# Involution weights made in the partition of their input column and copied from SBUF to SBUF, in a quantized-convolution and involution kernel

## The chip, the cores and the metric

The kernel runs on one core of a Trainium2 chip. The metric is the device time of one execution in microseconds; of three timed runs the median was 1388.15 us (1385.45 to 1391.19). The profile that this document quotes is one more execution, of 1388.26 us.

A core has a matrix engine (TensorE; the profile calls its matmuls PE and its loads of the stationary operand PEld), a vector engine (DVE), a scalar engine (ACT), GpSimd (POOL) and a queue engine (SP), each with its own instruction stream, and 16 DMA engines that all queues share. SBUF has 128 partitions; a matmul reads both operands from SBUF and writes PSUM. [...]

## The reference

The input is 32 images of 256 channels by 32 x 32 pixels, fp32. Two residual layers follow one another.

```python
# layer 0: group norm, 3x3 convolution with fp16-like quantization, bias, residual
x = x + _L0_conv_ref(_gn(x), weight, bias)
# layer 1: group norm, then an involution (7x7, 16 groups of 16 channels), residual
xn = _gn(x)
y = relu(bn(einsum('oc,bchw->bohw', w1, xn)))       # 64 features at each pixel
w = einsum('oc,bchw->bohw', w2, y) + b2             # 784 = 16 groups * 49 taps, at each pixel
patches = 7x7 neighbourhood of xn, zero padded
out = einsum('bgkhw,bgckhw->bgchw', w.reshape(b, 16, 49, 32, 32), patches)
x = x + out
```

The involution is a 7 x 7 convolution whose weights differ from pixel to pixel: each pixel has 49 weights for each of 16 groups, computed from its own 64 features `y`, and every channel of a group uses the same 49.

## The kernel before, in words

**The involution as a matmul.** The kernel turns the sum around: 128 *input* pixels (8 rows by 16 columns, one "side" of a block of 8 rows) stand on the partitions. The stationary operand is the input pixels' channels (`pixels`, a 64 x 32 corner of the array for each of two row halves and four groups), the moving operand is a "band": for each input pixel the weights with which it enters the output pixels around it. The matmuls of `sums` (line 517) add into PSUM tiles `acc`, and `add_windows` (line 533, DVE) adds these into the image in SBUF. An image has K = 4 blocks of 8 rows, each with SIDES = 2 sides of 16 columns, so 8 calls of `sums` of 32 matmuls each. Every fp32 matmul appears in the trace as two records, each with its own load.

**How a band comes about.** A weight is made where its *output* pixel is, and the band needs it where its *input* pixel is. `weights(b, r0)` (line 414) takes four rows of the image at a time: for each of them the 32 pixels' features are the stationary operand (64 features x 32 pixels), and two of the seven horizontal taps (224 columns of `w2_sb`; 112 for the last, single tap) are the moving operand. Four horizontal tap pairs fill the four 32-column strips of the array, and two rows its two 64-row halves, so eight such matmuls run side by side; a call has 16 matmuls (32 records) and an image eight calls. The result stands in PSUM with partition = strip of taps x column of the output pixel. `evict` (line 438, DVE, with the bias added) writes it into `w_sb`, a ring of 24 rows, 1920 instructions in all.

`scatter` (line 479) then sends each block of eight rows to DRAM: seven DMAs per block on SP's queue, each from 32 partitions, in pieces of 640 bytes, into the tensor `wd`, which is laid out by the column of the input pixel. `load_bands` (line 492) fetches the band of a block from there: 16 DMAs per block, each of 16 runs of 4512 bytes (70.5 KB), 14 of them issued by POOL and 2 by SP. The diagonal of the convolution (row r of the block shifts its weights by r) lies in the source's row step.

**The order of the work.** The whole order is written out by hand, in steps; an image has 16 of them. In step n, `front` of up to four later images advances by a stage (group norms on ACT and DVE, the 3x3 convolution on PE at line 336, nine matmuls a stage, then the features `y` through lines 384 and 391, and transposes into `pixels` at 399 and 403); on even steps follows `sums` of the current image and `weights` of a later one; on odd steps `add_windows`. Relative to the first `sums` of image b (step 0), `weights(b)` runs on the even steps -18 to -4 (`LEAD = 18`), the scatter of a block a step or two after its last rows, and `load_bands(b, k)` at step 4k - 9: the lag is 3 - 4 * NBAND with three band buffers. `sums` of the first side of a block waits for all DMAs of its band, so nothing on PE passes it.

**Queues.** POOL issues nothing but its share of the band loads. SP issues, in program order, image loads (line 108), scatters, its share of the band loads and stores (line 538). On each of the two queues a DMA waits for the eighth before it to land.

Of the kernel before, what the change touches and what calls it, by code (L numbers as in the profile page):

```python
# [9 lines left out]
F32 = mybir.dt.float32  # L10
AF = mybir.ActivationFunctionType
ALU = mybir.AluOpType

P = 128
B, C, H, W = 32, 256, 32, 32
N = H * W
# [41 lines left out]
S = H + 2 * PAD1  # L58
# [4 lines left out]
ROW = S * WPIX  # L63
WR = 4
NBAND = 3
SHARE = 8
NPIX = 6
RING = 24
FRONT = -56
LOAD = -63  # L70
LEAD = 18


@with_exitstack
def tile_quant_conv_then_involution(
# [23 lines left out]
    dram = ctx.enter_context(tc.tile_pool(name="dram", bufs=1, space=bass.MemoryType.DRAM))  # L99
# [43 lines left out]
    y_sb = [const.tile([P, N // 2], F32, name=f"y_{i}") for i in range(2)]  # L143
    bands = [const.tile([P, SIDES, WINC * WB + PAD], F32, name=f"band_{i}") for i in range(NBAND)]
    for t in bands[CH:]:
        nc.gpsimd.memset(t, 0.0)
    pixels = [const.tile([P, 2, PAIRS, PAIR], F32, name=f"pixels_{i}") for i in range(NPIX)]
# [4 lines left out]
    w_sb = const.tile([P, 2, RING, A, WIN, V], F32, name="w_sb")  # L152
    wd = dram.tile([H, S, WPIX], F32, name="wd")
# [4 lines left out]
    for kh in range(CH):  # L158
        wf = bands[kh].rearrange("p d n -> p (d n)")[:, : K0 * K0 * C].rearrange("p (k c) -> p k c", c=C)
        nc.sync.dma_start(wf, w0[kh * P : (kh + 1) * P])  # L160
        staged.append(wf)
# [3 lines left out]
    b2_sb = const.tile([P, 2, 2, SW], F32, name="b2_sb")  # L165
    for dj in range(K1):
        t, e = divmod(dj, 2)
        for r in range(2):
            nc.sync.dma_start(b2_sb[t * TW : (t + 1) * TW, e, r], b2[dj].partition_broadcast(TW))
# [19 lines left out]

    for col, cols, at, n in (  # L190
        (0, S, K1 * WB, PAD),
        (PAD1, PAD1, 0, PAD1 * WB),
        (W, PAD1, (K1 - PAD1) * WB, PAD1 * WB),
    ):
        to = bass.AP(
            tensor=wd.tensor,
            offset=wd.offset + col * WPIX + at,
            ap=[[ROW, H], [WPIX, cols], [1, n]],
        )
        nc.sync.dma_start(to, bands[NBAND - 1][:H, 0, :n].unsqueeze(1).to_broadcast([H, cols, n]))  # L200
# [87 lines left out]
    def front(b):  # L288
# [102 lines left out]
        nc.scalar.activation(y_sb[b % 2], py, AF.Relu, bias=bn_shift, scale=bn_scale)  # L391
# [14 lines left out]
    def weights(b, r0):  # L406

        pws = [ps_w.tile([P, 2, 2, SW], F32, tag=f"pw{i}", name=f"pw{i}") for i in range(2)]
        for r in range(2):
            for t in range(T):  # L410
                for i in range(2):
                    half = slice(i * CR, (i + 1) * CR)
                    dj = slice(2 * t, min(2 * t + 2, K1))
                    nc.tensor.matmul(  # L414
                        pws[i][t * TW : (t + 1) * TW, : dj.stop - dj.start, r],
                        y_sb[b % 2][half, (r0 // 2 + r) * W : (r0 // 2 + r + 1) * W],
                        w2_sb[half, dj],
                        start=True,
                        stop=True,
                    )  # L420
        for i in range(2):
            for e in range(2):
                p = P if e == 0 else (K1 // 2) * TW
                for r, rows, d0, d1, at in ring_pieces(b, r0 + 2 * i):
                    evict(pws[i][:p, e, r : r + rows], e, r, rows, d0, d1, at)

    def evict(of, e, r, rows, d0, d1, at):

        p = of.shape[0]
        to = w_sb[:p, e]  # L430
        to = bass.AP(
            tensor=to.tensor,
            offset=to.offset + at * WB + V * (K1 - 1 - d0),
            ap=[to.ap[0], [V * WIN, rows * A], [WB - V, d1 - d0], [1, V]],
        )
        of = of.rearrange("p r (a d v) -> p (r a) d v", a=A, v=V)
        bias = b2_sb[:p, e, r : r + rows].rearrange("p r (a d v) -> p (r a) d v", a=A, v=V)
        nc.vector.tensor_tensor(to, of[:, :, d0:d1], bias[:, :, d0:d1], ALU.add)  # L438

    def ring_pieces(b, r0):  # L440

        def place(r, d):
            s = r0 + r + d - PAD1
            return (b * H + s) % RING if 0 <= s < H else None

        def together(d):
            return place(0, d) is not None and place(1, d) == place(0, d) + 1

        pieces = []
        for rows, ok in (
            ((0, 2), together),
            ((0, 1), lambda d: place(0, d) is not None and not together(d)),
            ((1, 1), lambda d: place(1, d) is not None and not together(d)),
        ):
            d = 0
            while d < K1:
                d0 = d
                while d < K1 and ok(d) and place(rows[0], d) == place(rows[0], d0) + d - d0:  # L460
                    d += 1
                if d > d0:
                    pieces.append((*rows, d0, d, place(rows[0], d0)))
                else:
                    d += 1
        return pieces

    def scatter(b, k, part):

        at = (b * H + k * TR) % RING  # L470
# [161 lines left out]
```

## Time and profile before

| | before |
|---|---|
| timed runs, median (range) | 1388.15 us (1385.45 to 1391.19) |
| profiled execution: its own time, and the span of its instructions | 1388.26 us, 1386.5 us |
| PE / PEld busy | 1265.7 us (91%) / 809.6 us (58%) |
| DVE / ACT / POOL busy | 861.2 us (62%) / 727.1 us (52%) / 1010.0 us (73%) |
| DMA moved | 369.97 MB, 267 GB/s; queue shares 57.6% (SP) and 33.8% (POOL) of 16 engines |
| first and last start of `sums` (line 517) | 93.9 us and 1380.8 us |
| mean granted PE clock | 0.98 |

The page shows one execution on the chip. "Busy" of an engine counts its instructions' time; a group's line gives the source line, the engine, the shapes (output partitions x elements <- input), how often, its busy time and the mean of one in ns, and after the bar the idle time ahead of it and what ended that. Records of matmuls overlap, since each includes its way through the array, so the mean of one is longer than the pace at which they follow one another; the pace is read from the chain of the work that ended last, in order of time, which counts each stretch of time once. The share of a DMA queue is the time of its packets over the span of 16 engines.

### The profile page before, as it was taken

Reading aid. Unit: us, or ns where it says so; the run is one execution under the profiler, and the core shown is the slowest. Engines: PE = TensorE matmul, PEld = TensorE weight load, DVE = VectorE, ACT = ScalarE, POOL = GpSimd, SP = SyncE. Lnnn points to the kernel's source line nnn. Section 1 sums busy time; section 2 is a strip of 40 time slices with the busy share of each in tenths; the row PEclk is TensorE's granted clock in tenths of the full one; section 3 lists DMA queues with packets and bytes.
Section 4 is the critical chain, followed back from the end, with each engine's and each line's share of the span. In section 5 each row is a group of like instructions: output and inputs, shape, how many; then the busy total and the mean of one; then the engine's idle time right before and its main releaser. Section 6 shows DMA issues by size and latency. Waiting matters only on the chain.

```text
span 1386.5 us, 70020 instructions
## 1 busy us (share of the span) xinstructions
PE 1265.7 (91%) x29440; PEld 809.6 (58%) x29440; DVE 861.2 (62%) x3179; ACT 727.1 (52%) x1699; POOL 1010.0 (73%) x1818
## 2 busy tenths in 40 slices
PE   4799999999999999999999999999999998999763
PEld 2356666666665655566566666656666665656542
DVE  3366666666666666676676666657666675766542
ACT  4765555465646545665455565645556564553300
POOL 9067677687777777777768687777787767778785
PEclk9999999999999999999999999999999999999987
DMA  6089999999999999999999999999999999999995
GB/s 220 2 223 283 282 272 289 281 267 297 277 268 282 285 281 274 278 282 272 289 280 282 284 276 276 286 287 268 280 303 272 283 286 276 276 275 271 269 268 170
DMA packets 366568, 369.97 MB, mean 267 GB/s; under 512 B 78960, under 2 KB 308528, under 8 KB 366000
## 3 DMA queue, kind: packets, MB, share of 16 engines
q1 hardware_dynamic: 280240, 235.90, 57.6%
q0 software_dynamic: 86016, 129.60, 33.8%
q8 instruction: 234, 3.83, 1.2%
q14 instruction: 78, 0.64, 0.2%
HBM read 184.43 MB, written 180.76 MB: 263 GB/s over the span
## 4 chain that ended last, share of the span: by engine, by line
PE 58%; DMA 24%; POOL 5%; issue 4%; DVE 3%; ACT 3%; SPq 2%; POOLq 0%; DVEq 0%; ACTq 0%
PE pc L336 22%; PE acc L517 19%; DMA band<-wd 13%; PE pw L414 11%; DMA wd<-w_sb 9%; POOL band L492 5%; PE py L384 3%; PE pt L399 3%; DVE w_sb L438 2%; ACT junk L223 1%; SPq L479 1%; DMA w_sb<-in_w 1%; DVE x L533 0%; ACT xn L282 0%; DMA x<-in_x 0%
## 5 line engine op out<-in xcount | busy, mean ns | idle before, releaser
L492 POOL DMA_DIRECT2D band<-wd x1792 | 978.0, 548 | 363.0 <-DMA band<-wd 218.5
L438 DVE TENSOR_TENSOR w_sb<-pw,b_sb 128x16 f32<-128x16 f32 (+9 forms) x1920 | 373.7, 265 | 423.9 <-PE pw L414 403.5
L336 PE MATMUL pc<-xq,wq 128*128 128x496 f16 (+3 forms) x2304 | 535.8, 379 | 27.4 <-ACT xq L282 23.8
L517 PE MATMUL acc<-band,pixels 64*32 64x190 f32 (+1 forms) x16384 | 427.1, 330 | 68.5 <-DMA band<-wd 45.8
L336 PEld LDWEIGHTS <-wq 128*128 128x128 f16 x2304 | 206.8, 98 | 322.6 <-issue 110.1
L517 PEld LDWEIGHTS acc<-band,pixels 64*32 64x32 f32 x16384 | 301.7, 106 | 157.9 <-issue 86.1
L414 PE MATMUL pw<-w_sb,y 64*32 64x224 f32 (+1 forms) x8192 | 292.9, 332 | 17.0 <-issue 15.2
L533 DVE TENSOR_TENSOR x<-acc,x 128x380 f32<-128x380 f32 (+1 forms) x512 | 262.7, 513 | 32.8 <-PE acc L517 23.9
L414 PEld LDWEIGHTS pw<-w_sb,y 64*32 64x32 f32 x8192 | 187.7, 106 | 48.3 <-issue 31.1
L403 ACT COPY pixels<-pt 128x512 f32<-128x512 f32 x128 | 73.7, 576 | 237.5 <-PE pt L399 237.5
L223 ACT ACTIVATE junk<-x 128x512 f16<-128x512 f32 (+1 forms) x192 | 146.4, 763 | 20.1 <-DVE x L352 8.4
L223 ACT ACTIVATE junk<-x,mean 128x1024 f16<-128x1024 f32 x128 | 147.1, 1149 | 4.3
L254 ACT ACTIVATE s<-back,eps 128x2 f32<-128x2 f32 x64 | 18.9, 296 | 204.8 <-DVE back L239 204.7
L350 DVE TENSOR_SCALAR q<-pc 128x512 f16<-128x512 f32 x128 | 87.2, 682 | 19.3 <-PE pc L336 19.2
L282 ACT ACTIVATE xn<-x,off,rstd 128x512 f32<-128x512 f32 x128 | 96.2, 800 | 0.0
L352 DVE SCALAR_TENSOR_TENSOR x<-q,bias_sb,x 128x512 f32<-128x512 f16 x128 | 94.7, 740 | 0.3
L399 PEld LDWEIGHTS pt<-ident,xn 128*128 128x128 f32 x512 | 63.7, 142 | 25.9 <-issue 3.2
L399 PE MATMUL pt<-ident,xn 128*128 128x128 f32 x512 | 77.8, 275 | 0.1
L282 ACT ACTIVATE xq<-x,off,rstd 128x1024 f16<-128x1024 f32 x64 | 75.7, 1227 | 0.5 <-PE pc L336 0.5
L384 PEld LDWEIGHTS py<-xn,w_sb 128*64 128x64 f32 x2048 | 62.7, 138 | 16.6 <-issue 7.5
L244 ACT ACTIVATE mean<-back 128x2 f32<-128x2 f32 x64 | 12.7, 198 | 111.5 <-DVE back L239 111.4
L384 PE MATMUL py<-xn,w_sb 128*64 128x64 f32 x2048 | 67.6, 224 | 2.6 <-ACT xn L282 1.9
(40 smaller groups left out, 370.8 us busy)
## 6 DMA issues: line engine op xcount, KB each, us to landing
wd<-w_sb SPq DMA_DIRECT2D x896, 160.0 KB
band<-wd POOLq DMA_DIRECT2D x1792, 70.5 KB, 4.9
x<-in_x SPq DMA_DIRECT2D x64, 512.0 KB
out<-x SPq DMA_DIRECT2D x64, 512.0 KB
band<-wd SPq DMA_DIRECT2D x256, 70.5 KB
band<-in_w SPq DMA_DIRECT2D x2, 1152.0 KB
w_sb<-in_w SPq DMA_DIRECT2D x2, 196.0 KB
wd<-band SPq DMA_DIRECT2D x2, 180.0 KB
```

Source lines behind the costliest of these rows:

```text
L223: nc.scalar.activation(junk[:, n0:n1], src[:, h, n0:n1], func, bias=bias, accum_out=self.sums[:, i : i + 1])
L282: nc.scalar.activation(dst, src, AF.Identity, bias=self.off[:, one], scale=self.rstd[:, one])
L336: nc.tensor.matmul(pc.rearrange("p (r c) -> p r c", c=W)[:, r0 - nt * RT : r1 - nt * RT, c0:c1], wq[:, kh, k, mh * P : (mh + 1) * P], xq[: ...
L350: nc.vector.tensor_scalar(q, pc, F16_MAX, -F16_MAX, ALU.min, ALU.max)
L352: nc.vector.scalar_tensor_tensor(xt[:, mh, cols], q, bias_sb[:, mh : mh + 1], xt[:, mh, cols], ALU.add, ALU.add)
L384: nc.tensor.matmul(py[i * CR : (i + 1) * CR, cols], w1_sb[:, kh, :], px[:, r : r + 2], start=kh == 0, stop=kh == CH - 1,)
L399: nc.tensor.transpose(pt[:, i, h * P : (h + 1) * P], xn[:, h, (m + i) * P : (m + i + 1) * P], ident)
L414: nc.tensor.matmul(pws[i][t * TW : (t + 1) * TW, : dj.stop - dj.start, r], y_sb[b % 2][half, (r0 // 2 + r) * W : (r0 // 2 + r + 1) * W], w ...
L438: nc.vector.tensor_tensor(to, of[:, :, d0:d1], bias[:, :, d0:d1], ALU.add)
L492: queue.dma_start(band[j::JC, :, j * WB : j * WB + WPIX], src)
L517: nc.tensor.matmul(at[t * TW : (t + 1) * TW, h, :, f - top : l - top], px[p, a, v * GC : v * GC + TW], of[:, :, a, f - top : l - top, v], ...
L533: nc.vector.tensor_tensor(x_at, of, x_at, ALU.add)
```

## The change

**Features shifted instead of weights.** The partition of a weight is now that of its *input* pixel from the start. For input pixel column j, the weight of horizontal tap dj is that of the output pixel at column j - dj + 3; so the features `y` are stored with three zero columns on either side, and the stationary operand of a matmul is a window of them that is shifted by dj. The taps of `w2` and `b2` are reversed to suit. The layout of `y` puts the image's four blocks of eight rows next to each other, so that one stationary operand holds 128 pixels: one row of each of the four blocks, all 32 columns (64 features x 128 pixels).

**An image at a time.** For each row position rho around a block (-3 to 10), and each of the seven dj, one matmul makes the weights of those vertical taps, d0 to d1, that fall into the block: the moving operand has (d1 - d0) * 16 columns, 16 to 112. That is 98 matmuls an image, 49 in each 64-row half of the array, in pairs that run in both halves. They are dealt out to eight units of 14, 7, 4, 10, 4, 3, 4 and 3 pairs (`UNITS`), at the steps 0, 2, 4, 6, 8, 10, 12 and 13 after -18 (`STEPS`): the last unit stands at step -5, one step earlier than the last call did. All four bands of an image need all eight units. The eviction writes 128 partitions, in 20 instructions an image, into `w_sb`, which now holds two images and no ring.

**No DRAM.** The scatter and `wd` are gone. `load_bands` copies from SBUF to SBUF: 32 DMAs per block, each from *one* partition (8 rows of 4512 bytes, 36 KB) to eight partitions, half of them issued by SP and half by POOL.

**What pays for the room.** Two bands instead of three (so `load_bands(b, k)` is issued at step 4k - 5), bands that share their columns between the two sides, and a smaller scratch area for the descriptors that POOL writes.

```diff
-S = H + 2 * PAD1
+BLK = 8
+QB = H // BLK
+YW = (W + 2 * PAD1) * QB
+YR = BLK // 2
-NBAND = 3
-SHARE = 8
+SCRATCH = 4096
+NBAND = 2
+SHARE = 2
-RING = 24
+UNITS = (
+    ((-3, 0, 7), (8, 0, 7)),
+    ((0, 0, 7),),
+    ((1, 0, 4),),
+    ((1, 4, 7), (9, 0, 7)),
+    ((5, 0, 4),),
+    ((5, 4, 7),),
+    ((4, 0, 4),),
+    ((4, 4, 7),),
+)
+STEPS = (0, 2, 4, 6, 8, 10, 12, 13)
...
-    y_sb = [const.tile([P, N // 2], F32, name=f"y_{i}") for i in range(2)]
-    bands = [const.tile([P, SIDES, WINC * WB + PAD], F32, name=f"band_{i}") for i in range(NBAND)]
+    y_sb = [const.tile([P, YR * YW + 2 * QB], F32, name=f"y_{i}") for i in range(2)]
+    bands = [const.tile([P, (WINC + WINI) * WB + PAD], F32, name=f"band_{i}") for i in range(NBAND)]
...
-    w_sb = const.tile([P, 2, RING, A, WIN, V], F32, name="w_sb")
-    wd = dram.tile([H, S, WPIX], F32, name="wd")
+    w_sb = const.tile([P, 2, BLK, WPIX], F32, name="w_sb")
...
-        nc.scalar.activation(y_sb[b % 2], py, AF.Relu, bias=bn_shift, scale=bn_scale)
+        to = y_sb[b % 2][:, QB : QB + YR * YW].rearrange("p (r c k) -> p r c k", r=YR, k=QB)[:, :, PAD1 : PAD1 + W]
+        of = py.rearrange("p (k r c) -> p r c k", r=YR, c=W)
+        nc.scalar.activation(to, of, AF.Relu, bias=bn_shift, scale=bn_scale)
...
+    def weights(b, n):
+        pws = [ps_w.tile([P, NT], F32, tag=f"pw{i}", name=f"pw{i}") for i in range(2)]
+        parts = [[], []]
+        muls = [[], []]
         for i in range(2):
+            at = 0
+            for rho, j0, j1 in UNITS[n]:
+                rho = BLK - 1 - rho if i else rho
+                d0, d1 = max(0, PAD1 - rho), min(K1, BLK + PAD1 - rho)
+                cols = (d1 - d0) * G
+                parts[i].append((at, rho, j0, j1, d0, d1))
+                for dj in range(j0, j1):
+                    muls[i].append((at, rho, dj, d0, d1))
+                    at += cols
+        for both in zip(*muls):
+            for i, (at, rho, dj, d0, d1) in enumerate(both):
+                half = slice(i * CR, (i + 1) * CR)
+                k, r = divmod(rho, BLK)
+                y0 = QB + (r // 4 * 2 + r % 2) * YW + dj * QB + k
+                nc.tensor.matmul(
+                    pws[i][:, at : at + (d1 - d0) * G].rearrange("p (a n) -> p a n", a=A),
+                    y_sb[b % 2][half, y0 : y0 + P],
+                    w2_sb[half, dj].rearrange("p (a n) -> p a n", a=A)[:, :, V * d0 : V * d1],
+                    start=True,
+                    stop=True,
+                )
+        for i in range(2):
+            for part in parts[i]:
+                evict(b, pws[i], *part)
...
+    def load_bands(b, k):
+        band = bands[(b * K + k) % NBAND]
+        for i in range(W):
+            d, j = i // JC, i % JC // 2 + i % 2 * JC // 2
+            w = w_sb[(d * JC + j) * QB + k : (d * JC + j) * QB + k + 1, b % 2]
+            src = bass.AP(
+                tensor=w.tensor,
+                offset=w.offset,
+                ap=[w.ap[0], [WPIX - V, TR], [1, WPIX]],
+            )
+            at = (j if d else WINI + j) * WB
+            to = band[j::JC, at : at + WPIX]
+            if i % SHARE == SHARE - 1:
+                nc.sync.dma_start(to, src)
+            else:
+                nc.gpsimd.dma_start(to, src)
...
-            if b is not None and i % 2 == 0:
-                weights(b, i // 2 * WR)
-
-            for part in range(2):
-                b, i = due(n, -LEAD + 1 + part)
-                if b is not None and i % 2 == 0:
-                    for k in range(K):
-                        if i // 2 == min((k + 1) * TR // WR, H // WR - 1):
-                            scatter(b, k, part)
+            if b is not None and i in STEPS:
+                weights(b, STEPS.index(i))
...
-    nc = bacc.Bacc("TRN2", target_bir_lowering=False, num_devices=1)
+    nc = bacc.Bacc("TRN2", target_bir_lowering=False, num_devices=1, dynamic_dma_scratch_size=SCRATCH)
```

The new `evict` differs from the old one in its strides alone: with d = d1 - d0 and q = 8 (j1 - j0), it adds `b2_sb` to 128 partitions of q * d pairs and writes these into the image's half of `w_sb`.

## The prediction, made before the changed kernel was run

> **What bounds the kernel now.** I read the page's busy shares first, then its chain, then the chain in order of time, then PE's waits.
>
> ```profile
> PE 1265.7 (91%) x29440; PEld 809.6 (58%) x29440; DVE 861.2 (62%) x3179; ACT 727.1 (52%) x1699; POOL 1010.0 (73%) x1818
> ...
> q1 hardware_dynamic: 280240, 235.90, 57.6%
> q0 software_dynamic: 86016, 129.60, 33.8%
> ```
>
> PE and the DMA engines (57.6% + 33.8%) are both near full, so the shares don't say which sets the time. The chain in order of time does:
>
> ```profile
> 980.13 2.01 PE pc L336 x9
> 982.14 2.02 PE py L384 x64
> 984.16 1.51 PE acc L517 x44
> 985.67 0.76 PE pw L414 x15
> 986.43 2.01 PE pc L336 x9
> 988.44 1.50 PE acc L517 x39
> ```
>
> It runs on PE, each piece starting where the last one ended; columns are start, length, work. An image is eight times (acc 1.50 + pw 0.75 + pc 2.01) = 34.1 us, plus py 2.02 and four stretches of pt. From the first `sums` (93.9) to the last (1380.8) an image takes 1286.9 / 32 = 40.2 us. So a microsecond of PE work per image costs 32 us, unless it falls into a wait. The waits on transfers are few:
>
> ```profile
> PE acc L517 <- DMA band<-wd: 45.8, 21, 7.5
> PE acc L517 <- DMA wd<-w_sb: 5.5, 1, 5.5
> ```
>
> That is 51 us in total (total, times, longest), all that lighter DMA can give back to PE directly, though the chain puts 24% of the span down to DMA: most of that lies beside a busy PE.
>
> **Weights on PE.** `weights` costs 0.75 us a call in the chain, 8 x 0.75 = 6.0 us an image. The streams explain it: two rounds, two records each, of 224 columns are 896 columns in 0.75 us, 0.84 ns a column; eight tiles run side by side, and a load of only 32 columns hides under 188 ns of streaming. After, 49 pairs of matmuls stand in two tiles of 64 x 128. Streaming shrinks a little: 3136 columns x 2 records x 0.84 = 5.3 us. But each record now needs its own load of 128 fp32 columns, and streams only 16 to 112. What does such a load take?
>
> ```profile
> L384 PE MATMUL py<-xn,w_sb x2048: 216/222/271, 56.3 to 1302.8; 128*64 128x64 f32 x187
> L414 PE MATMUL pw<-w_sb,y x32: 256/349/373, 61.1 to 61.7; 64*32 64x224 f32 x24, 64*32 64x112 f32 x8
> 631.56 0.60 PE L399 MATMUL pt<-ident,xn 128*128 128x128 f32 x4
> 632.09 1.41 PE L517 MATMUL acc<-band,pixels 64*32 64x133 f32 x60
> 60.77 0.38 PE L336 MATMUL pc<-xq,wq 128*128 128x496 f16 x1
> 61.09 0.98 PE L414 MATMUL pw<-w_sb,y 64*32 64x224 f32 x32
> ```
>
> The first two (by line: minimum/median/maximum) give the load where it lies bare, in the first record after a change of shape: 271 - 222 = 49 ns for 64 columns, 373 - 349 = 24 ns for 32 (the window of one call, the first). It grows by 25 ns per 32 columns, so 98 ns for 128. The next two (timeline) give the nearest shape: four records of pt, each a 128-column fp32 load and 128 columns of stream, in 632.09 - 631.56 = 0.53 us, of which 0.1 is the change of shape: 107 ns each. The change itself is in the last two: pc's last record starts at 60.77 and streams 2.01 / 9 = 0.22, pw starts at 61.09, 0.10 later. I take 107 ns a record, as nearest in shape; longest stream 112 x 0.84 = 94, so the load is always the longer. Both tiles load side by side: in that first call the eight tiles, two to each strip, show the same 373. An image: 98 x 0.107 = 10.5, and per unit 0.10 to enter the shape, which `weights` shared with `sums` before, and 0.07 for the last stream: 8 x 0.17 = 1.4. Together 11.9 us in place of 6.0: **+5.9 us, x 32 = +187 us**. Bounds: with loads hidden entirely 5.3 + 1.4 = 6.7, +22 us; with the tiles loading in turn (196 x 0.107 + 1.4 = 22.4), +525 us.
>
> [...]
>
> **Waits on transfers that go.** wd is written and read no more: 143 MB out and 147 in become 148 MB inside SBUF. The 51 us go: **-51 us**. Bounds 0 (another stall takes their place) and -51.
>
> **The last unit and the first band.** The wait that comes is this one. Until now block 0's band was fetched as soon as its rows were scattered. After, all 32 DMAs of (b, 0) wait for DVE's eviction of unit 7, at step -5, and the first `sums` of the image for all 32. On PE there stand between: py 2.02, sums 1.50, pc 2.01, sums 1.50, unit 0 of the next image (14 pairs, 28 x 0.107 + 0.17 = 3.2), pc 2.01: 12.2 us. On the other side:
>
> ```profile
> L438 DVE TENSOR_TENSOR w_sb<-pw,b_sb 128x224 f32<-128x224 f32 x256 | 98.1, 383 | 187.8 <-PE pw L414 184.7 <-DMA wd<-w_sb 3.0
> L438 DVE TENSOR_TENSOR w_sb<-pw,b_sb 128x64 f32<-128x64 f32 x64 | 13.7, 215 | 19.1 <-PE pw L414 18.7
> L492 POOL DMA_DIRECT2D band<-wd x1792: 547/547/683, 77.8 to 1372.9; - x200
> L492 SPq DMA_DIRECT2D band<-wd x256: 570/592/2219, 79.3 to 1361.6; - x128
> DMA to landing us min/median/max: 2.4/4.9/8.8
> ```
>
> Eviction: (383 - 215) / 160 = 1.05 ns an element, 148 fixed; unit 7 has two of 336 elements, 1.0 us, and 0.2 to wake. Then fifteen issues ahead of the last: 8.2 us on POOL at 547, 8.9 on SP at 592; the number of runs per DMA halves, so these are upper bounds (SP's scatters went at 302). Then landing, 2.4 to 4.9 us. Sum 11.8 to 15.0 against 12.2: PE waits 0 to 2.8 us an image, 0 to 87 us. With half the data per DMA and half the load I stand near the lower end: 0.8 us, **+25 us**. The bands k = 1 to 3 wait for `sums` of band k - 2 instead; from the end of `sums` 1 to the start of `sums` 4 lie three rounds of acc, pw, pc with pt, over 14 us even before units grew: nothing.
>
> **Queues.** POOL: 2048 DMAs at most 547 are 1120 us, 8.75 us a band against 45.9 / 4 = 11.5. SP loses 896 scatters and has 2048 band DMAs, 9.5 us a band at 592; loads of x, 63 steps ahead, queue behind them; the store ahead of band k = 1 makes SP wait for one `add_windows` (two of 513 ns), within that band's slack. Eight in flight a queue at 0.55 allow 4.4 us to land. Nothing, as long as DMAs land so; cover gone, see the third rival.
>
> **DVE, ACT, start.** 1920 evictions (374 us) become 640: 640 x 0.148 + 200,704 elements x 1.05 ns = 305 us. DVE is at 62%, and a unit has two steps of some 2.5 us to be emptied (unit 7 one, with pc and py between): nothing. y's 32 strided writes (769 ns each) lie stages ahead of use: nothing. w_sb's clearing grows with its columns from 6.5 to 15.3 us on POOL, long before the first weights at 61 us: nothing.
>
> **Sum.** Against the profiled execution's own 1388.3 us (0.1 above the median): 1388.3 + 187 - 51 + 25 = **1549, say 1550 us**, 12% slower. With loads at 98 ns it would be 1521; with the late band at 0 or 87 us, 1524 to 1611.
>
> **Rivals.**
> *Loads hide, nothing is late.* 1388 + 22 - 51 = 1359 us, 2% faster. For it: before, every load hid, and the waits on bands are real. Against it: 49 and 24 ns bare, and pt's 107. It decides where a record costs under 65 ns: 98 x 0.065 + 1.4 = 7.7, +54 us against the -51. 0.09.
> *Loads hide, the first band is late.* Unit 0 shrinks by 1.3 us, and PE's way to step 0 with it, to 10.9: the wait is 0.9 to 4.1 us, 28 to 127 us, so 1387 to 1486, middle 1435. 0.13.
> *One partition is too slow a source.* Every band DMA reads 36 KB from one partition; before, it read DRAM, and a scatter read 32 partitions. No row has one. The windows at the first scatters, with no band load yet, show what few partitions yield (DMA share and GB/s last):
>
> ```profile
> 71.00:72.50 1.50, 1.50 (x38) 0.82 (x37) 0.78 (x3) 1.37 (x3) 0.00 (x0) 1.00 0.89 186
> 72.70:73.70 1.00, 1.00 (x7) 0.44 (x6) 1.00 (x5) 1.00 (x2) 0.00 (x0) 1.00 1.01 270
> ```
>
> The first DMAs, from partitions 0 to 63, keep the engines 89% busy at 186 GB/s; when 64 to 127 join it is 270. So where the bytes stand limits. At worst a partition gives its share of 32, 186 / 32 = 5.8 GB/s: with sixteen in flight 93 GB/s, 12.4 us for the 1155 KB of a band, 128 x 12.4 + 95 = 1.68 ms. If a queue's DMAs went one at a time it would be worse, above 3 ms. Against it: neighbours in a queue read different partitions, and 102 GB/s would do. 0.18, half of it under 1.72 ms.
>
> [...]
>
> **How the numbers follow.** Forecast 0.60 (1500 to 1640), and 0.09, 0.13 and 0.18 as above. Low 1420 leaves out the first rival and a third of the second (0.04); high 1720 leaves out half of the third, 0.09. A change of under 0.5% (1381 to 1395) can't be told from none: same 0.03, from the second rival's edge; faster 0.09; slower 0.88.
>
> **What will show it.** `weights` on the chain at 0.21 us a pair, some 10 to 12 us an image, PEld busy through it; no DMA ahead of `sums` but at each image's first, under 2 us; DMA share near half; DVE near 790 us. I am wrong if a pair takes under 0.13 us (loads hide), if the waits ahead of all four bands grow (one partition too slow: landing above 5 us, queues waiting for their own DMAs), or if the granted clock falls below 0.96 during the sparse units.

## The result and the profile after

The changed kernel takes **1859.05 us** (median of 4 runs, 1852.52 to 1872.09) against 1387.31 us before: 1.341 times as long, with a 95% interval of 1.333 to 1.349. Forecast were 1550 us and a range of 1420 to 1720. The direction was right, the size was not: 472 us more, where 162 were forecast. Three executions of the experiments below, one of lead20's and two of both20's, took over 1.5% longer than the fastest of the same kernel and are left out of the medians.

The page of the changed kernel: busy time, granted clock (tenths, 40 slices), busy share of the DMA engines, and the two DMA queues (packets, MB, share of 16 engines).

```profile
PE 1612.6 (87%) x27520; PEld 1109.0 (60%) x27520; DVE 777.4 (42%) x1899; ACT 734.6 (40%) x1699; POOL 1121.6 (60%) x2075
...
PEclk9988899988889988889988889988889888888776
DMA  4077666676766667666677766667667667666665
...
q1 hardware_dynamic: 61168, 144.34, 34.8%
q0 software_dynamic: 65536, 74.12, 30.4%
```

The queues move 222.6 MB in place of 370 and yet hold the DMA engines for 65% of a longer span. The granted clock of TensorE, 0.98 on average before, is 0.875. DVE is at 777 us, as forecast (790).

The chain in order of time, around the first sums of an image (start, length, work):

```profile
924.94 3.26 PE pw L424 x56
928.20 2.02 PE pc L332 x9
930.22 0.23 issue
930.45 2.12 POOL band L465 x4
932.57 3.30 DMA band<-w_sb
935.88 2.79 PE acc L490 x49
938.66 3.18 PE pw L424 x28
941.84 3.88 PE pc L332 x9
...
946.56 1.52 PE acc L490 x44
948.09 1.05 PE pw L424 x16
949.14 2.01 PE pc L332 x9
```

Three things can be read here. A unit of weights with 14 pairs (L424 x56) costs 3.26 us for 28 records a tile, as the prediction had it (3.2). PE stands still from 930.2 to 935.9 for the first band. And after that wait the same sums take 2.79 us in place of 1.5 and the same conv 3.88 in place of 2.0: TensorE runs at half speed for 10 us. The stretches show it (busy time by engine, then granted clock, DMA share, GB/s):

```profile
924.90:930.20 5.30, 5.30 (x69) 3.97 (x65) 1.84 (x5) 1.13 (x1) 4.72 (x9) 1.00 0.65 90
930.20:935.90 5.70, 0.04 (x5) 0.06 (x6) 1.03 (x2) 1.24 (x1) 5.52 (x12) 0.73 0.88 181
935.90:945.70 9.80, 9.80 (x102) 6.56 (x103) 2.71 (x5) 0.00 (x0) 3.05 (x6) 0.50 0.67 138
945.70:955.40 9.70, 9.70 (x203) 7.40 (x202) 3.03 (x9) 4.37 (x9) 6.24 (x12) 0.96 0.80 179
```

With the matmul records and the clock records of a trace the whole span can be split, from 95 us to the last matmul: idle (no matmul runs), lost to the clock (half of the time in which matmuls ran at half clock), and the rest, PE's work at full clock. The table also has the experiments of the next section whose split is used there; their names are explained there. The time is the median of the timed runs, the split that of the profiled execution, which is up to 15 us away from it (contig: 1712.72 us); noband, late0 and perm were timed once each:

| kernel | time, us | idle | lost at half clock | PE work at full clock |
|---|---|---|---|---|
| before | 1387 | 88 | 15 | 1183 |
| **after** | 1859 | 211 | 200 | 1345 |
| lead20 | 1840 | 250 | 133 | 1352 |
| noband | 1483 | 8 | 18 | 1356 |
| late0 | 1750 | 415 | 71 | 1163 |
| contig | 1727 | 163 | 95 | 1353 |
| perm | 1864 | 279 | 137 | 1346 |
| split20 | 1858 | 257 | 145 | 1351 |
| both20c | 1649 | 107 | 83 | 1357 |
| k0only | 1762 | 146 | 167 | 1345 |
| k0perm | 1825 | 255 | 118 | 1345 |
| late0b | 1530 | 190 | 68 | 1170 |

From before to after: PE's work +162, idle +123, clock +185, together 470, the difference of the two spans (1856.7 - 1386.5). The forecast had +187, -26 and nothing. So work was about right, 149 us of waits and 185 us of clock were missed.

The waits of PE ahead of `sums` (total, times, longest), to set beside the two lines shown of before:

```profile
PE acc L490 <- DMA band<-w_sb: 145.6, 56, 10.1
...
PE acc L490 <- DMA out<-x: 59.3, 15, 6.2
```

The second names a store of x, which `sums` don't read; 14 of its 15 waits stand ahead of first bands, behind whose DMAs SP issues stores (at 931.92 in the image shown), so these waits too are taken to be for bands. By the matmul records, PE idles ahead of the sums of the first band of an image for 121 us in all (14 before), of the second 29 (19), the third 42 (12), the fourth 17 (11). The first band's DMAs in the timeline (start, length of the run of issues, engine):

```profile
918.73 13.15 SPq L463 DMA_DIRECT2D band<-w_sb  x16
919.00 3.72 POOL L465 DMA_DIRECT2D band<-w_sb  x7 [7.46 <-DVE w_sb L447]
...
924.92 4.25 POOL L465 DMA_DIRECT2D band<-w_sb  x8 [2.21 <-issue]
```

SP needs 13.15 us for sixteen issues (12.0 on average over all bands), where 592 ns each would be 9.5: some issues, 560 ns at the median, take up to 2465. POOL pauses after its seventh, but is done with its sixteenth at 930.26, before SP (931.88); the "POOL band x4" of the chain above belongs to the next band. That both queues are held by their own transfers is an inference: for POOL the profile names them over all bands (below), for this pause it names nothing, and for SP the experiments with another source speak for it.

```profile
POOL band L465 <- DMA band<-w_sb: 119.0, 158, 2.9
```

### The profile page after: what moved, and what is told of

Read it like the earlier page. It is cut to its first block, busy times and chain, and to the rows that moved or that the text cites. A ratio compares the mean times of both kernels' runs of the same rounds, so it can differ in the third digit from the quotient of the medians.

```text
span 1856.7 us, 64838 instructions
## 1 busy us (share of the span) xinstructions
PE 1612.6 (87%) x27520; PEld 1109.0 (60%) x27520; DVE 777.4 (42%) x1899; ACT 734.6 (40%) x1699; POOL 1121.6 (60%) x2075
## 4 chain that ended last, share of the span: by engine, by line
PE 53%; SPq 19%; DMA 14%; POOL 7%; issue 3%; DVE 2%; ACT 1%; POOLq 0%; ACTq 0%
PE pc L332 19%; SPq L463 19%; PE acc L490 16%; PE pw L424 15%; DMA band<-w_sb 11%; POOL band L465 7%; DMA out<-x 3%; PE pt L397 2%; DVE w_sb L447 1%; DMA band<-in_w 1%; PE py L380 1%; DMA x<-in_x 0%; ACT junk L219 0%; SPq L511 0%; DVE q L346 0%
## 5 line engine op out<-in xcount | busy, mean ns | idle before, releaser
L465 POOL DMA_DIRECT2D band<-w_sb x2048 | 1089.0, 534 | 714.0 <-PE acc L490 292.6
L447 DVE TENSOR_TENSOR w_sb<-pw,b_sb 128x448 f32<-128x448 f32 (+7 forms) x640 | 277.4, 480 | 904.5 <-PE pw L424 890.8
L490 PE MATMUL acc<-band,pixels 64*32 64x190 f32 (+1 forms) x16384 | 458.1, 352 | 208.4 <-DMA band<-w_sb 145.6
L332 PE MATMUL pc<-xq,wq 128*128 128x496 f16 (+3 forms) x2304 | 605.4, 415 | 26.2 <-ACT xq L278 24.6
L490 PEld LDWEIGHTS acc<-band,pixels 64*32 64x32 f32 x16384 | 329.2, 114 | 302.6 <-issue 257.1
L424 PEld LDWEIGHTS pw<-w_sb,y 64*128 64x128 f32 x6272 | 424.6, 211 | 99.4 <-issue 66.4
L424 PE MATMUL pw<-w_sb,y 64*128 64x16 f32 (+5 forms) x6272 | 466.2, 299 | 3.8 <-DVE w_sb L447 3.0
L332 PEld LDWEIGHTS <-wq 128*128 128x128 f16 x2304 | 222.7, 105 | 307.1 <-issue 108.8
L397 PEld LDWEIGHTS pt<-ident,xn 128*128 128x128 f32 x512 | 70.1, 153 | 28.7 <-issue 8.9
L380 PE MATMUL py<-xn,w_sb 128*64 128x64 f32 x2048 | 67.0, 224 | 0.5 <-ACT xn L278 0.5
L380 PEld LDWEIGHTS py<-xn,w_sb 128*64 128x64 f32 x2048 | 62.4, 138 | 4.4 <-ACT xn L278 0.7
L389 ACT ACTIVATE y<-py,bn_shift,bn_scale 128x512 f32<-128x512 f32 x32 | 24.9, 778 | 80.2 <-PE py L380 80.1
```

The lines of the kernel that those rows point to most:

```text
L332: nc.tensor.matmul(pc.rearrange("p (r c) -> p r c", c=W)[:, r0 - nt * RT : r1 - nt * RT, c0:c1], wq[:, kh, k, mh * P : (mh + 1) * P], xq[: ...
L380: nc.tensor.matmul(py[i * CR : (i + 1) * CR, cols], w1_sb[:, kh, :], px[:, r : r + 2], start=kh == 0, stop=kh == CH - 1,)
L397: nc.tensor.transpose(pt[:, i, h * P : (h + 1) * P], xn[:, h, (m + i) * P : (m + i + 1) * P], ident)
L424: nc.tensor.matmul(pws[i][:, at : at + (d1 - d0) * G].rearrange("p (a n) -> p a n", a=A), y_sb[b % 2][half, y0 : y0 + P], w2_sb[half, dj]. ...
L447: nc.vector.tensor_tensor(to, of, bias, ALU.add)
L465: nc.gpsimd.dma_start(to, src)
```

## The experiments

**1. What do the weights units cost by themselves?** The bands are not carried (noband).

```diff
-            if b is not None and i % 4 == 0:
+            if b == 0 and i in (0, 4):
                 load_bands(b, i // 4)
```

> The bands are loaded for the first two blocks alone; all later sums run on what lies in the bands. This leaves out the carrying of the weights, so PE never waits for a band, and what is left over the kernel before is the price of the weights units. If a record costs its load, 107 ns, as the prediction had it: 1388 - 86 (all idle time of PE ahead of matmuls before) + 187 = 1490, between 1470 and 1510 us, with the granted clock at 0.97 or more. If the sparse units lower the clock by themselves: above 1580 us with the clock under 0.92. If loads hide: under 1340 us.

Measured: 1483.45 us (one run), clock 0.985. The units in its chain:

```profile
908.91 3.26 PE pw L424 x56
912.17 2.01 PE pc L332 x9
914.18 1.54 PE acc L490 x53
915.72 1.71 PE pw L424 x28
...
921.39 1.05 PE pw L424 x16
```

x56, x28 and x16 are matmuls of both tiles, so 28, 14 and 8 records a tile; a record of the x56 unit streams 16 or 48 columns, of the x28 unit 64, of the x16 unit 80. (3.26 - 1.05) / (28 - 8) = 0.11 us a record, whatever it streams, and 0.17 a unit on top: so the stream is not the price. The load, the same in all of them, is what is left; records of L380, which load 64 columns, go faster (64 in 2.02 us, here 56 in 3.26). The eight units are 12.2 us an image, where 11.9 were forecast. The units alone do not lower the clock, and with the bands gone PE idles 8 us and loses 18 to the clock in place of 211 and 200: the waits and the lost clock of the changed kernel both come with the carrying of the bands. And 1483 us is a floor: even if the bands came for nothing, this change would be 7% slower than the kernel before.

**2. Is it the eviction of unit 7 that holds the first band back?** All units are made two steps earlier (lead20).

```diff
-LEAD = 18
+LEAD = 20
```

> All eight units of weights are made two steps earlier, so that the eviction of unit 7 is no longer what the first band of an image waits for; nothing else is changed. Theory A (the wait ahead of an image's first sums halves the TensorE clock for some 10 us): PE's idle time ahead of the first sums falls from 121 us to under 50, the time at half clock from 465 us to under 200, and the whole to 1600 to 1680 us. Theory B (the sparse weights units, two tiles of 64 x 128 with 16 to 112 columns, halve the clock by themselves): the idle time goes, the time at half clock stays above 350 us, and the whole is 1720 to 1780 us.

Measured: 1840.30 us, 1.334 times before (1.325 to 1.344), above what both theories expected. The wait ahead of the first band's sums is nearly gone (121 to 7 us), but not the waiting: 156 us now stand ahead of the second band's. Waits of this kernel (total, times, longest):

```profile
POOL band L465 <- PE acc L490: 545.8, 115, 11.0
PE acc L490 <- DMA band<-w_sb: 209.8, 74, 9.9
```

So the gate forecast was there, but behind it the bands are late anyway: with two buffers, band k may start when `sums` of band k - 2 end (POOL's 545.8), and its carrying takes longer than PE's way to band k. Theory A was half right: time at half clock fell from 457 to 324 us (both from 95 us on), and the idle time moved.

**3. Is one partition a slow source?** Every band DMA reads its eight rows from eight partitions, four apart (spread), or from eight neighbouring ones (contig); number, bytes, queues and destinations stay, and other weights reach the bands.

```diff
-            w = w_sb[(d * JC + j) * QB + k : (d * JC + j) * QB + k + 1, b % 2]
...
-                ap=[w.ap[0], [WPIX - V, TR], [1, WPIX]],
-            )
+            p0 = i % 2 * (P // 2) + i // 2 % 4
+            src = w_sb[p0 : p0 + 4 * TR : 4, b % 2, i % BLK]
```

That was spread; contig has, in the same place:

```diff
+            p0 = i % 2 * (P // 2) + i // 2 % 4 * TR
+            src = w_sb[p0 : p0 + TR, b % 2, i % BLK]
```

> Each band DMA reads its eight rows of 4512 B from eight partitions, four apart, in place of one; number, size, queues and destinations of the DMAs are the same. Which weights reach the bands is changed by it. Theory C (one partition is a slow source): the 4512 B packets fall from medians of 373 and 482 ns to about 200, SP issues the sixteen DMAs of a band in 9 us in place of 12, PE's idle time ahead of sums falls from 202 us to under 80, and the whole to 1540 to 1640 us. Theory D (the issue of sixteen DMAs on each queue and the landing of the last set the band's 16 to 17 us, whatever the source): the packets, the wait and the whole stay, 1820 to 1870 us.

> As in the run that read eight partitions four apart, but the eight partitions lie next to each other, so that units of weights have no new wait for band DMAs. Which weights reach the bands is changed by it. Theory C (one partition is a slow source): packets of 4512 B at 180 to 250 ns in place of 482 and 373, SP's sixteen issues in 9 to 10 us in place of 12.0, 2 to 3 us from the last issue to the sums in place of 3.5, PE's idle time ahead of sums under 80 us in place of 202, the whole 1520 to 1640 us. Theory D (sixteen issues a queue and two buffers for the bands set the pace, whatever the source): idle time above 150 us and the whole above 1760 us.

Measured: spread 2249.75 us, slower than the changed kernel, against both theories. The edit had made a wait of its own: the units' evictions now waited for band DMAs, which took 1094 us of DVE's time.

```profile
DVE w_sb L447 <- DMA band<-w_sb: 1094.4, 110, 12.9
```

Its packets still answer the question. The median packet of 4512 bytes took, on POOL's queue and SP's, 482 and 373 ns from one partition (changed kernel), 334 and 269 ns from eight neighbours, 181 and 179 from eight partitions four apart, and 181 and 178 in the kernel before, out of DRAM. Contig, without that wait, took 1727.47 us, 1.248 times before (1.240 to 1.256): 132 us less than the changed kernel, by the source alone. In the profiled executions 48 us of the gain are idle time and 106 clock. SP's issues of the changed kernel and of contig (minimum/median/maximum ns):

```profile
L463 SPq DMA_DIRECT2D band<-w_sb x2048: 559/560/2465, 92.5 to 1842.5; - x187
```
```profile
L459 SPq DMA_DIRECT2D band<-w_sb x2048: 564/564/1758, 92.5 to 1698.5; - x187
```

The mean fell from 703 to 592 ns, a band's sixteen from 12.0 to 10.5 us. Theory C names one cause, and not the only one: idle time stayed at 163 us, which is above the 150 that Theory D asked for, and 1727 us lie between the two theories (1640 at most for C, over 1760 for D). Against the run without bands contig still loses 244 us.

**4. Do the two queues meet at one place of SBUF?** SP takes the second side first (flip; with the earlier units, flip20).

```diff
             d, j = i // JC, i % JC // 2 + i % 2 * JC // 2
+            d = i % 2 ^ d
```

> Only the order of the band DMAs on SP's queue is changed: SP takes its eight columns of the second side first and those of the first side after, while POOL keeps the first side first. Until now the two queues, at the same place in their order, read partitions 32 apart; after, partitions 64 and more apart. All sixteen DMAs of each queue, their sizes and destinations stay. [...] Theory C2 (one partition is slow whatever the other queue reads): nothing moves, 1830 to 1870 us.

> The changed order on SP's queue together with all units two steps earlier. If the source is what made the bands late and the eviction of unit 7 what held the first one back, the two together leave little to wait for: PE's idle time ahead of sums under 60 us, the clock above 0.96, the whole 1500 to 1580 us. If flip alone changes nothing, this gives what the earlier units gave alone, 1820 to 1860 us.

Measured: 1867.80 us (ratio 1.337 to 1.355) and 1845.85 us (1.330 to 1.340), as without the edit; had the two queues been in each other's way, flip was to take 1650 to 1780 us. Flip's packets took 481 ns on POOL's queue, as before the edit, and 327 on SP's, down from 373, which the time does not show. What the other queue reads at the same place is not it; that leaves the eight rows of one DMA out of one partition, as experiment 3 has them.

**5. Is SP's queue the bottleneck?** With the earlier units, 12 DMAs a band on SP and 20 on POOL (split20); the store of an image's second half and the load of x a step later (store20); both (both20).

```diff
-            if i % SHARE == SHARE - 1:
+            if i % 8 in (1, 4, 7):
```
```diff
-LOAD = -63
+LOAD = -62
...
-                if i // 2 == M - 1:
-                    store(b, 1)
-                    x_tiles.pop(b)
...
+            b, i = due(n, 2)
+            if b is not None and i == 2 * (M - 1):
+                store(b, 1)
+                x_tiles.pop(b)
```

> All units two steps earlier, and of the 32 DMAs of a band 12 on SP's queue and 20 on POOL's, in place of 16 and 16. Theory G (SP's queue is what the bands wait for: 16 issues at a mean of 0.66 to 0.70 us, four times an image, behind stores and loads of x, are 46 of the image's 54 us): twelve issues take 8 to 9 us, SP is no longer late at the bands, POOL's twenty take 11 to 12 us, PE's idle time ahead of sums falls from 242 us (units earlier, 16 and 16) to under 140 and the whole from 1844 to 1600 to 1720 us. Theory H (the single source sets the pace of the sum of both queues): the twenty on POOL slow down as SP's did, the idle time stays above 200 us and the whole above 1800 us.

> All units two steps earlier, 16 and 16 DMAs, and only the store and the load of x one step later. If what makes the second band late is the store ahead of its DMAs on SP's queue, the idle time ahead of the second band's sums falls from 156 us to under 80 and the whole from 1844 to 1720 to 1790 us; if SP's queue is full anyway, the wait moves to another band and the whole stays at 1810 to 1850 us.

> As the run with 12 and 20, and SP's store of an image's second half and its load of x one step later, so that they stand behind the band DMAs of their step and not ahead of them. Theory G: SP begins the second band of an image when its buffer comes free, the idle time ahead of its sums (156 us with the units earlier) falls under 60 us, the whole 1540 to 1680 us, and below the run with 12 and 20 alone. Theory H: within 1% of the run with 12 and 20 alone.

Measured: 1857.53, 1925.36 and 1862.15 us (both20: 1.330 to 1.357 times before). Theory G falls. With four DMAs fewer, each of SP's got slower: 816 ns an issue on average in place of 657 (lead20), so that twelve took 10.7 us where sixteen had taken 11.6, and POOL's twenty took 12.7. The carrying of a band takes its 12 us in both, and both20 is within 1% of split20, as Theory H expected. But 10.7 of POOL's 12.7 us are its own twenty issues at 535 ns, so the split does not show that the source sets the pace of both queues together. The later store alone (store20) made it worse through a wait that I had not seen: the load of x now stood right behind the store whose buffer it takes, and SP waited for that to land, with the third band's DMAs behind it. SP's wait in store20:

```profile
SPq L120 <- DMA out<-x: 119.9, 27, 5.2
```

**6. Everything proposed taken away at once.** both20 with the source of contig (both20c; `p0` and `src` as above).

> The run with 12 and 20, the later store and the earlier units, and every band DMA reading eight neighbouring partitions in place of one, which changes the weights that reach the bands. All causes of waits that are proposed are taken away here, and only the units of weights stay dearer than before: if the list is complete, PE's idle time ahead of sums is under 50 us, the clock 0.97 or more, and the whole 1483 (no bands carried) plus at most 50 us, 1485 to 1535 us. If it stays above 1600 us, a cause is missing.

Measured: 1649.15 us, 1.190 times before (1.179 to 1.201). Against both20 only the source differs: 213 us. SP's issues in split20 and in both20c:

```profile
L463 SPq DMA_DIRECT2D band<-w_sb x1536: 559/588/3109, 94.7 to 1834.8; - x192
```
```profile
L459 SPq DMA_DIRECT2D band<-w_sb x1536: 564/564/1699, 95.0 to 1625.2; - x192
```

SP's twelve now take 7.7 us, POOL's twenty 11.5. But 107 us of idle time and 83 lost at half clock remain. The list was not complete: the run is 114 us above the upper end that was expected. POOL's own twenty issues and the two buffers may be what is missing; no run takes these apart.

**7. Is the first band late by itself, or by its neighbours?** Only the first band of each image is carried (k0only).

```diff
-            if b is not None and i % 4 == 0:
+            if i == 0 or (b, i) == (0, 4):
                 load_bands(b, i // 4)
```

> Of the bands, only the first of each image is carried (and the second of the first image); later sums run on what lies in the bands, so three quarters of the traffic are left out, and the queues are empty when the first band is asked for. Theory C (the band's own transfer out of single partitions is late): SP's sixteen issues still take 11 to 12 us and the last lands 3 us or more after its issue, PE waits 2 to 4 us ahead of the first sums of each image, 64 to 130 us in all, and with the time at half clock the whole is 1600 to 1720 us against 1483 without any band. Theory I (neighbouring traffic made it late, as the prediction's sum for this wait would have it): sixteen issues in 9 us, under 50 us of idle time, the whole under 1545 us.

Measured: 1761.74 us (1.244 to 1.285 times before). POOL had waited 43 us for the eviction, no other band was in the queues, and still:

```profile
942.17 12.04 SPq L463 DMA_DIRECT2D band<-w_sb  x16
942.43 4.80 POOL L465 DMA_DIRECT2D band<-w_sb  x9 [43.14 <-DVE w_sb L447]
```

Sixteen issues took 12.4 us on average, another 3.8 passed to the sums, the packets were no faster than with all bands (558 and 466 ns on POOL's and SP's queue), and PE waited 4.5 us an image, 143 us in all. So it is the band's own transfer, and Theory I falls. The whole is 278 us over the run without bands, 138 of them idle time and 149 clock, which is more than I had expected (1720 us at most).

**8. Why does the clock stay low for 10 us?** In the kernel before, the first band is asked for later, for a long wait beside dense units (late0) and for one of about the changed kernel's length (late0b); in the changed kernel, the units are put in another order, in full (perm) and with the first band alone (k0perm).

```diff
             b, i = due(n, 3 - 4 * NBAND)
-            if b is not None and i % 4 == 0:
+            if b is not None and i % 4 == 0 and i:
                 load_bands(b, i // 4)
+            b, i = due(n, -3)
+            if b is not None and i == 0:
+                load_bands(b, 0)
```

Late0b takes `i in (8, 12)` in the first of these lines and asks for `load_bands(b, 1)` after `load_bands(b, 0)`. The other order of the units:

```diff
 UNITS = (
+    ((5, 4, 7),),
+    ((4, 4, 7),),
     ((-3, 0, 7), (8, 0, 7)),
     ((0, 0, 7),),
-    ((1, 0, 4),),
     ((1, 4, 7), (9, 0, 7)),
+    ((1, 0, 4),),
     ((5, 0, 4),),
-    ((5, 4, 7),),
     ((4, 0, 4),),
-    ((4, 4, 7),),
 )
```

> The kernel before, with the first band of each image asked for six steps later (step -3 in place of -9), so that PE waits some 3 to 6 us at each image's first sums, with the dense weights of before. Theory A (a wait of that length halves the clock, whatever the weights): about 100 to 190 us of idle time and 3.4 to 10 us at half clock in most images, the time at half clock above 150 us and the whole 1560 to 1700 us. Theory B (it takes the sparse units): the idle time alone, 1480 to 1570 us, with the clock above 0.96.

> The kernel before, with the first and the second band of each image asked for at step -3, the first band first, for a wait of some 3 to 7 us ahead of the first sums, with the dense weights units of before. Theory E: the clock is at half for 5 us or less after the wait, as in the run with the 12 us wait. Theory F: some 10 us, as in the changed kernel.

> The eight units are made in another order: the two smallest (three shifts, 6 records a tile, 96 or 112 columns each) come first, around the first sums of an image, and the two with the shortest streams come third and fourth. Theory E (sparse units beside the wait keep the clock low after it): after a wait the clock stays at half for 3 to 6 us in place of 10, the time at half clock falls from 465 us to under 330; the wait itself may grow by up to 2.4 us an image, as there is less work ahead of the first sums. Theory F (the wait alone sets the time at half clock): 10 us after a wait as before, half clock at 450 us or more, the whole at 1858 us or above.

> The same, with the units in the other order (the two smallest first, around the first sums of an image). The wait ahead of the first sums grows by about 2.4 us, as there is less work ahead of it. Theory E (sparse units beside the wait keep the clock low): after the wait the clock stays at half for 3 to 7 us in place of some 10, although the wait is longer. Theory F (the wait alone): 10 us or more.

Measured, with the median wait ahead of PE (waits over 1.5 us, the last images left out) and the time that the clock stayed at half after it:

| kernel | time, us | wait, us | half clock after it, us |
|---|---|---|---|
| late0 (before, dense units) | 1750.31 | 11.8 | 4.1 |
| late0b (before, dense units) | 1529.97 | 4.4 | 3.8 |
| k0only (28 records of 16 or 48 columns before the wait, 14 of 64 after) | 1761.74 | 3.9 | 9.7 |
| k0perm (6 records of 96 or 112 columns on each side) | 1824.56 | 7.5 | 4.2 |
| perm (the same) | 1864.14 | 7.0 | 6.6 |

The chain after one such wait in k0only, k0perm and late0b:

```profile
589.59 2.79 PE acc L490 x50
592.38 3.18 PE pw L424 x28
595.56 3.88 PE pc L332 x9
```
```profile
550.04 2.79 PE acc L490 x49
552.83 1.55 PE pw L424 x12
554.39 2.01 PE pc L332 x9
```
```profile
548.98 2.15 PE acc L517 x41
551.74 1.16 PE pw L414 x12
552.90 2.01 PE pc L336 x9
```

In k0only conv still runs at half speed (3.88); in the other two it is back at 2.01. The medians hide groups: the clock stayed at half for 7.5 us or more after 28 of k0only's 30 waits, but also after 8 of k0perm's 29 and 12 of perm's 29. A wait of the same length, 3.9 and 4.4 us, is followed by 9.7 us at half clock beside sparse units and by 3.8 beside dense ones, and a longer wait with the small units at it by 4.2. Theory F, the wait alone, falls; Theory E agrees in direction. Why the units beside the wait make that difference, no run shows. The reordered units gained nothing in time: with less work ahead of the sums the idle time grew by as much as the clock gave back in perm (68 and 63 us), by more in k0perm (109 and 49), and perm's 409 us at half clock and 6.6 us after a wait are above the 330 and the 6 that were expected.

Late0's wait came out at 12 us, not the 3 to 6 it was set for, since the second band's DMAs stood ahead of the first's; late0b mends that.

## Why the prediction was wrong

**Weights on PE: right.** +187 forecast; PE's work at full clock grew by 162, and by 173 in the run without bands. A record cost 0.110 us and a unit 0.17 more, where 0.107 and 0.17 were used; the difference lies in the 6.0 us an image put down for the units before (by the matmul records, each stretch of time counted once at full clock, they took 6.6, and the units after 11.7). The rivals in which loads hide are out: 0.110 us a record were measured in noband, over units that stream 16 or 48, 64 and 80 columns.

**The last unit and the first band: mechanism right, size wrong.** Of the sum's parts, PE's way to the sums (12.2; 12.5 in the image shown) and the landing (2.4 to 4.9; 4.2 at the median from SP's last issue to the sums) held. The fifteen issues ahead of the last did not: 8.9 us at most on SP were 11.5 on average. They were taken from rows whose DMAs read DRAM, and called upper bounds because the number of runs halves; what a run costs when eight of them come out of one partition was not in them. With eight neighbouring partitions (contig) the fifteen took 9.4 us. I had named the unknown, as the third rival, and then left it out of this term. The wait is 3.8 us an image in place of 0.8. (The 0.2 us to wake is in no row, and no run shows it; in the image shown SP's first issue starts 0.03 us after the last eviction has ended (918.70), POOL's 0.30 us after it.)

The row was misread as well. Its 592 ns is a median; the 256 issues of SP in it take 192.6 us by the trace, 753 ns on average and 2219 at most, so issues on SP stretched in the kernel before too, and fifteen at that mean are 11.3 us. The 302 ns given for SP's scatters is the minimum of a row with a median of 524. A sum over a run of issues needs the mean.

**Waits that go: wrong.** I took the end at which all 51 us go. The lower end of 0, "another stall takes their place", was nearer: ahead of the bands k = 1 to 3 PE idles 87 us, 42 before. (The 143 MB written to wd are 147 by the page; nothing rests on it.)

**Queues: wrong.** "Nothing, as long as DMAs land so" was the condition, and they didn't: a packet of 4512 bytes took 482 and 373 ns in place of 181 and 178, and SP's sixteen issues 12.0 us a band in place of 9.5.

**The third rival was the case, in part.** Of the 376 us that the changed kernel needs over the run without bands, the single partition explains 132 (contig; 213 between both20 and both20c); how the other 244 divide among the number of issues, the two buffers and the clock behind their waits stays open. The rival's worst estimate, one partition giving its share of 32 and a band taking 12.4 us, is near what SP's queue needed (12.0), but with eight partitions it still needed 10.5, so this is no proof of the share. Half of the rival's chance was put above the range, and the result lies there. 1.68 ms was its time without any loss to the clock; 1859 less the 185 us that the clock took more than before is 1674; as the waits are also those of two buffers, the closeness of the two is luck.

Why eight neighbouring partitions are a slower source than eight that lie four apart (334 and 269 ns a packet against 181 and 179), no run shows.

**The clock: left out.** I named a fall of the clock as a thing that could prove me wrong, for the sparse units alone, and gave it no price. The units alone don't do it (0.985 in noband), and a wait beside dense units costs less: late0b lost 68 us to the clock over 190 us of idle time, late0 71 over 415. The two together lost 200 us over 211, 185 more than before, which is more than the weights units themselves cost.

The clock records of the two kernels change in steps of 3.41 us (their lengths are multiples of it but for each trace's last one). Beside dense units the clock was back 3.8 us after the wait (late0b), beside sparse ones 9.7 us after it (k0only), about three such steps; in the changed kernel's stretch at half clock shown above, PE was busy for all of its 9.80 us.

## What to carry to other kernels

Price a DMA inside SBUF by the partitions that its bytes come from, not by bytes or by the rows of a DMA out of DRAM: a packet of 4512 bytes took 482 ns on POOL's queue and 373 on SP's here from one partition, over twice the 181 and 179 from eight that lie four apart. Price a run of issues by the mean of its row, not by the median. When a change thins the work around a wait on TensorE, price the wait with the half-clock time behind it, which in k0only was longer than the wait (9.7 us after 3.9). And count stationary loads when tiles grow: that term could be read off the profile to 15% (187 us forecast, 162 measured).

## What was not expected of the hardware

- The time of a DMA issue on SP differs with the source and with what stands on the queue: 0.56 us at the median, 703 ns on average with a single-partition source, up to 2.5 us, and 816 when SP had fewer of them (split20); 592 with eight neighbouring partitions, and 753 in the kernel before, where its band loads read DRAM and stood among scatters. That issues stretch with the transfers ahead of them is inferred from this. POOL's issues stay at 534 ns at the median (667 at most), and POOL waits between them instead, 119 us for its own band DMAs.
- Half clock for 9.7 us after a wait of 3.9 us beside sparse units (k0only), and for 3.8 us after one of 4.4 beside dense ones (late0b).
- Some waits as short as 2.2 to 2.8 us beside the sparse units were followed by 10 us at half clock in the changed kernel (at 216, 1045 and 1209 us); one of 2.5 us at 1238 us was followed by none.
